# Two GIN layers on sorted edges: sums of six edge chunks in PSUM and masked adds in SBUF, in place of scatter-adds to DRAM

## Chip, core and metric

The kernel runs on one core of a Trainium2 chip. Its engines work side by side, each through its own queue in order: PE (TensorE, with its weight loads shown as PEld), DVE (VectorE), ACT (ScalarE), POOL (GpSimd) and SP (SyncE, which here only issues DMAs). DMAs are issued by SP, ACT and POOL, and the data is moved by 16 DMA engines. The metric is the device time of one execution in microseconds (us); lower is better.

## The reference

A graph with 6250 nodes and 100000 edges. Each of two layers adds to every node the rows of the nodes that have an edge to it, then applies two dense layers. At the end stand a residual and a layernorm. Everything is float32.

```python
# x [6250, 256], src and dst [100000]; dst is sorted
dst = jnp.minimum((6250 * jax.random.uniform(key, (100000,)) ** 2.0).astype(jnp.int32), 49999)
_o = jnp.argsort(dst, stable=True); src = src[_o]; dst = dst[_o]

def _gin_agg(h, src, dst, eps, n_nodes):
    agg = jax.ops.segment_sum(h[src], dst, num_segments=n_nodes)
    return (1.0 + eps) * h + agg

h = _gin_agg(x, src, dst, eps1, n)          # width 256
h = jax.nn.relu(h @ W1a + b1a)              # 256 -> 512
h = jax.nn.relu(h @ W1b + b1b)              # 512 -> 512
h = _gin_agg(h, src, dst, eps2, n)          # width 512
h = jax.nn.relu(h @ W2a + b2a)              # 512 -> 512
x = _layernorm(x + h @ W2b + b2b)           # 512 -> 256
```

The destinations are squares of uniform numbers times 6250, so low node numbers have many edges and high ones few.

## The kernel before

The edges are cut into 782 chunks of 128, one edge in each partition. Edge p * 782 + c stands in partition p of chunk c, so the 128 edges of a chunk are far apart in the list. The program has four stages, one behind the other: aggregate, mlp, aggregate, mlp.

**aggregate** (L171) works on four chunks (GRP) at a time. For each chunk, POOL issues an indirect DMA that gathers the 128 source rows from DRAM into a tile g (L176), six chunks (AHEAD) ahead of their use. PE transposes the chunk's destinations into a PSUM tile pt (L189), and DVE compares them with themselves to get a selection matrix sel (L193): 1 where two edges share a destination. PE multiplies sel with g into pm (L215), which adds up the rows of a chunk that share a destination. ACT copies pm to m (L217), and POOL issues a second indirect DMA that adds m to an accumulator in DRAM (L218); only the first edge of a destination adds to the true row, the others go to spare rows. Which row each edge adds to is worked out on DVE in the first aggregation (L201 to L209) and used again in the second. There are four accumulators (NACC) per layer, so that scatters can overlap.

**mlp** (L225) takes 512 nodes (BLK) at a time: SP loads the four accumulators' rows (part, L235), DVE adds them up (L238), PE transposes them (L241), and the two matrix products follow (ph at L249, po at L258). In the first layer the result goes to DRAM as h1 (L269), and, scaled, as the seed of the second accumulator (L272). In the second come residual and layernorm (L274 to L290).

Before the first aggregation the accumulators are filled: SP writes the seeds (L142), and ACT issues the zero fills (L115, L121) for all accumulators of both layers. ACT's copies at L217 stand behind these issues in ACT's queue. x stays in SBUF for the seed and the residual.

The order within each engine's queue is set by the framework's scheduler from the order in the code, the tile pools' buffer counts (bufs) and the dependences.

Of the kernel before, what the change touches and what calls it, by code (L numbers as in the profile page):

```python
# [11 lines left out]
ALU = mybir.AluOpType  # L12

P = 128
NACC = 4    # independent accumulators in DRAM, so that scatter-adds overlap
# [3 lines left out]
EPS_LN = 1e-5  # L19


@with_exitstack
def tile_gin_residual_layernorm(
# [32 lines left out]
    PAD = N                         # the row to which padding edges add  # L56
    ROWS = -(-(N + 1 + P) // P) * P  # nodes, padding row, a spare row per partition
# [3 lines left out]
    edge = ctx.enter_context(tc.tile_pool(name="edge", bufs=3))  # L61
    dense = ctx.enter_context(tc.tile_pool(name="dense", bufs=2))
    psum = ctx.enter_context(tc.tile_pool(name="psum", bufs=2, space=bass.MemoryType.PSUM))

    acc1 = [dram.tile([ROWS, D], F32, name=f"acc1_{k}") for k in range(NACC)]
    acc2 = [dram.tile([ROWS, H], F32, name=f"acc2_{k}") for k in range(NACC)]
    h1 = dram.tile([N, H], F32, name="h1")

# [1 line left out]
    srcs = const.tile([P, NCH], I32, name="srcs")  # L70
    dsti = const.tile([P, NCH], I32, name="dsti")
    nc.gpsimd.memset(srcs, 0)
    nc.gpsimd.memset(dsti, PAD)
    full = E // NCH
    for t, a in ((srcs, src), (dsti, dst)):
        nc.sync.dma_start(t[:full], a[: full * NCH].rearrange("(p c) -> p c", c=NCH))
        if E > full * NCH:
            nc.sync.dma_start(  # L78
                t[full : full + 1, : E - full * NCH],
                a[full * NCH :].rearrange("(p c) -> p c", p=1),  # L80
            )
# [3 lines left out]
    before = const.tile([P, P], F32, name="before")  # 1 where column < partition  # L85
    nc.gpsimd.memset(before, 1.0)
    nc.gpsimd.affine_select(
        out=before, in_=before, pattern=[[-1, P]], compare_op=ALU.is_gt, fill=0.0,
        base=0, channel_multiplier=1,
    )  # L90
    spare = const.tile([P, 1], F32, name="spare")
    nc.gpsimd.iota(spare, pattern=[[0, 1]], base=N + 1, channel_multiplier=1,
                   allow_small_or_imprecise_dtypes=True)

    dstf = const.tile([P, NCH], F32, name="dstf")
    nc.vector.tensor_scalar(dstf, dsti, float(PAD), None, op0=ALU.min)  # L96
    move = const.tile([P, NCH], F32, name="move")    # from the destination to the spare row
    nc.vector.tensor_scalar(move, dstf, -1.0, spare, op0=ALU.mult, op1=ALU.add)
    rows = const.tile([P, NCH], I32, name="rows")    # the row to which an edge adds

# [6 lines left out]
    zeros = const.tile([P, 1600], F32, name="zeros")  # L107
    nc.vector.memset(zeros, 0.0)

    def zero(acc, width):  # L110
        flat = acc.rearrange("(p r) d -> p (r d)", p=P)
        total = ROWS // P * width
        for o in range(0, total, 1600):
            n = min(1600, total - o)
            nc.scalar.dma_start(flat[:, o : o + n], zeros[:, :n])  # L115

    def zero_spare(acc, width):
        n = ROWS - N
        for r in range(0, n, P):
            m = min(P, n - r)  # L120
            nc.scalar.dma_start(acc[N + r : N + r + m, :], zeros[:m, :width])  # L121

    xs = const.tile([P, NT, D], F32, name="xs")
    for n0 in range(0, N, BLK):
        nb = min(BLK, N - n0)
        t0 = n0 // P
        g = nb // P
        if g:
            nc.sync.dma_start(
                xs[:, t0 : t0 + g, :], x[n0 : n0 + g * P, :].rearrange("(t p) d -> p t d", p=P)  # L130
            )
        if nb > g * P:
            nc.sync.dma_start(xs[: nb - g * P, t0 + g, :], x[n0 + g * P : n0 + nb, :])

    zero_spare(acc1[0], D)
    for a in acc1[1:]:
        zero(a, D)
    for t in range(NT):
        m = min(P, N - t * P)
        s = dense.tile([P, D], F32, tag="seed1", name="seed1", bufs=3)  # L140
        nc.vector.tensor_scalar(s[:m], xs[:m, t, :], e1[:m, 0:1], None, op0=ALU.mult)
        nc.sync.dma_start(acc1[0][t * P : t * P + m, :], s[:m])  # L142

# [1 line left out]
    def weight(w, kk, width, name):  # L145
        t = const.tile([P, kk, width], F32, name=name)
        nc.sync.dma_start(t, w.rearrange("(k p) f -> p k f", p=P))
        return t
# [17 lines left out]
    for a in acc2[1:]:  # L166
        zero(a, H)
    zero_spare(acc2[0], H)

# [1 line left out]
    def aggregate(table, width, accs, find_rows):  # L171
        gathered = {}

        def gather(c):
            g = edge.tile([P, width], F32, tag="g", name="g", bufs=AHEAD + 2)
            nc.gpsimd.indirect_dma_start(  # L176
                out=g, out_offset=None, in_=table,
                in_offset=bass.IndirectOffsetOnAxis(ap=srcs[:, c : c + 1], axis=0),
            )
            gathered[c] = g  # L180

        for c in range(min(AHEAD, NCH)):
            gather(c)
        for c0 in range(0, NCH, GRP):
            n = min(GRP, NCH - c0)
            cs = slice(c0, c0 + n)
            pt = psum.tile([P, GRP, P], F32, tag="pt", name="pt")
            for i in range(n):
                nc.tensor.transpose(  # L189
                    pt[:, i, :], dstf[:, c0 + i : c0 + i + 1].to_broadcast([P, P]), ident  # L190
                )
            sel = edge.tile([P, GRP, P], F32, tag="sel", name="sel")
            nc.vector.tensor_tensor(  # L193
                sel[:, :n, :], pt[:, :n, :], dstf[:, cs].unsqueeze(2).to_broadcast([P, n, P]),
                op=ALU.is_equal,
# [14 lines left out]
            for i in range(n):  # L210
                c = c0 + i
                if c + AHEAD < NCH:
                    gather(c + AHEAD)
# [111 lines left out]
```

## Time and profile before

| | |
|---|---|
| timed runs, median of 3 | 5891.14 us (5888.76 to 5893.97) |
| profiled execution, its span | 5891.6 us |
| busy: PE, DVE, ACT, POOL | 3258.7, 876.9, 864.8, 4031.6 us |
| moved by DMA | 802.48 MB, 136 GB/s over the span |
| gathers and scatters (software queue q0) | 325312 packets, 615.19 MB |
| mean granted TensorE clock | 0.601 of full speed |

The page of the profile shows the span in 40 slices, with each engine's busy share in tenths; the groups of instructions by line give count, mean duration in ns, and the idle time ahead of them with what ended it. The timeline lists instructions in order of time, with the idle time of the engine ahead of each. A matrix product in float32 appears as two MATMUL records. The granted clock is the share of full speed that the hardware gave TensorE.

### The profile page before, as it was taken

How to read it: one execution, taken by the hardware profiler on the slowest of the kernel's cores; microseconds unless marked ns; L12 is line 12 of the kernel's file. 1: busy time of each engine (PE TensorE's matmuls, PEld its weight loads, DVE VectorE, ACT ScalarE, POOL GpSimd, SP SyncE). 2: the span in 40 equal slices, each digit the busy share in tenths (PEclk: the TensorE clock that was granted, in tenths of full speed). 3: DMA queues.
4: the chain of work that ended last, by engine and by line, in shares of the span. 5: the costliest groups of instructions: out<-in, count | busy, mean ns of one | idle time of the engine just before them, and what ended most of it. 6: DMA issues, size and time to landing. Idle time of an engine off the chain costs nothing.

```text
span 5891.6 us, 29066 instructions
## 1 busy us (share of the span) xinstructions
PE 3258.7 (55%) x6394; PEld 1396.1 (24%) x6394; DVE 876.9 (15%) x3186; ACT 864.8 (15%) x1768; POOL 4031.6 (68%) x3139
## 2 busy tenths in 40 slices
PE   0244444444444444446976666666666666666688
PEld 0122222222222222222432222222222222222254
DVE  1011111111111111112410000000000000000354
ACT  0011111111111111111211111111111111111111
POOL 0388888888888888883038888888888888888300
PEclk7555555555555555557986666655666655655699
DMA  7855555555555555555559999999999999999753
GB/s 275 289 82 82 82 83 83 82 83 82 82 82 82 83 82 83 82 82 137 185 135 166 165 165 165 165 165 165 166 165 166 165 165 165 166 165 165 182 170 112
DMA packets 430637, 802.48 MB, mean 136 GB/s; under 512 B 62132, under 2 KB 206768, under 8 KB 430466
## 3 DMA queue, kind: packets, MB, share of 16 engines
q0 software_dynamic: 325312, 615.19, 60.7%
q1 hardware_dynamic: 71740, 93.57, 5.3%
q10 hardware_dynamic: 33414, 91.86, 4.0%
q8 instruction: 56, 0.92, 0.1%
q14 instruction: 115, 0.94, 0.1%
HBM read 395.04 MB, written 405.34 MB: 136 GB/s over the span
## 4 chain that ended last, share of the span: by engine, by line
DMA 66%; issue 13%; PE 8%; POOL 7%; DVE 3%; ACT 1%; SPq 1%; ACTq 0%; POOLq 0%; DVEq 0%
DMA g<-in_x_dram,srcs 34%; DMA g<-h,srcs 18%; DMA acc<-m,rows 7%; POOL acc L218 5%; DMA part<-acc 4%; PE pm L215 4%; PE po L258 3%; PE ph L249 2%; POOL g L176 2%; DMA acc<-seed 2%; DVE part L238 1%; DMA acc<-zeros 1%; ACT m L217 1%; DMA xs<-in_x_dram 0%; SPq L78 0%
## 5 line engine op out<-in xcount | busy, mean ns | idle before, releaser
L215 PE MATMUL pm<-g,sel 128*128 128x256 f32 (+1 forms) x3128 | 2352.0, 854 | 2464.0 <-DMA g<-in_x_dram,srcs 1377.6
L218 POOL DMA_INDIRECT acc<-m,rows x1564 | 2462.9, 1575 | 648.9 <-issue 332.0
L215 PEld LDWEIGHTS pm<-g,sel 128*128 128x128 f32 x3128 | 751.4, 298 | 3776.5 <-ACT m L217 3397.8
L217 ACT COPY m<-pm 128x256 f32<-128x256 f32 (+1 forms) x1564 | 748.5, 479 | 4213.5 <-DMA acc<-m,rows 2903.9
L176 POOL DMA_INDIRECT g<-h,srcs x782 | 771.6, 987 | 550.9 <-issue 471.8
L176 POOL DMA_INDIRECT g<-in_x_dram,srcs x782 | 794.6, 1016 | 279.8 <-DMA g<-in_x_dram,srcs 125.3
L193 DVE TENSOR_TENSOR sel<-pt,dstf 128x512 f32<-128x512 f32 x392 | 270.2, 690 | 4450.1 <-PE pm L215 4439.7
L189 PE MATMUL pt<-ident,dstf 128*128 128x128 f32 x1564 | 406.8, 413 | 53.0 <-DVE dstf L96 51.5
L189 PEld LDWEIGHTS pt<-ident,dstf 128*128 128x128 f32 x1564 | 338.7, 225 | 323.0 <-issue 301.3
L238 DVE TENSOR_TENSOR part<-part 128x256 f32<-128x256 f32 (+2 forms) x294 | 163.6, 557 | 335.0 <-DMA part<-acc 331.6
L249 PE MATMUL ph<-zt,w2a_s 128*128 128x512 f32 (+1 forms) x416 | 191.8, 623 | 12.7 <-DVE zt L244 12.7
L201 DVE SCALAR_TENSOR_TENSOR scr<-sel,before 128x128 f32<-128x128 f32 x782 | 181.6, 287 | 6.6
L258 PE MATMUL po<-w1b_s,ht 128*128 128x512 f32 (+1 forms) x392 | 172.3, 597 | 3.5 <-DVE h1t L266 3.5
L249 PEld LDWEIGHTS ph<-zt,w2a_s 128*128 128x128 f32 x416 | 83.2, 209 | 114.7 <-issue 98.5
L258 PEld LDWEIGHTS po<-w1b_s,ht 128*128 128x128 f32 (+1 forms) x392 | 74.7, 191 | 98.4 <-issue 92.3
L258 PE MATMUL po<-w2b_s,ht 128*128 128x256 f32 (+1 forms) x392 | 90.8, 389 | 6.6 <-DVE y L276 6.6
L241 PE MATMUL pt<-ident,part 128*128 128x128 f32 (+1 forms) x294 | 49.2, 295 | 80.6 <-DVE part L238 47.3
L249 PE MATMUL ph<-zt,w1a_s 128*128 128x512 f32 (+1 forms) x208 | 89.2, 582 | 4.7 <-DVE zt L244 4.7
L258 PEld LDWEIGHTS po<-w2b_s,ht 128*128 128x128 f32 (+1 forms) x392 | 76.1, 195 | 24.2 <-DVE y L276 8.2
L253 ACT ACTIVATE ht<-ph,b2a_s 128x512 f32<-128x512 f32 (+1 forms) x52 | 34.4, 661 | 202.1 <-PE ph L249 188.4
L201 DVE DVE_READ_ACCUMULATOR scr<-sel,before 128x1 f32 x782 | 63.6, 81 | 0.0
L241 PEld LDWEIGHTS pt<-ident,part 128*128 128x128 f32 (+1 forms) x294 | 34.3, 147 | 101.5 <-issue 57.5
(34 smaller groups left out, 412.6 us busy)
## 6 DMA issues: line engine op xcount, KB each, us to landing
acc<-zeros ACTq DMA_DIRECT2D x72, 800.0 KB
part<-acc SPq DMA_DIRECT2D x192, 256.0 KB
acc<-m,rows POOLq DMA_INDIRECT x1564
part<-acc SPq DMA_DIRECT2D x192, 128.0 KB
g<-in_x_dram,srcs POOLq DMA_INDIRECT x782
g<-h,srcs POOLq DMA_INDIRECT x782
h<-h1r ACTq DMA_DIRECT2D x48, 256.0 KB
acc<-seed ACTq DMA_DIRECT2D x48, 256.0 KB
```

Of the source, the lines that this page charges most:

```text
L176: nc.gpsimd.indirect_dma_start(out=g, out_offset=None, in_=table, in_offset=bass.IndirectOffsetOnAxis(ap=srcs[:, c : c + 1], axis=0),)
L189: nc.tensor.transpose(pt[:, i, :], dstf[:, c0 + i : c0 + i + 1].to_broadcast([P, P]), ident)
L193: nc.vector.tensor_tensor(sel[:, :n, :], pt[:, :n, :], dstf[:, cs].unsqueeze(2).to_broadcast([P, n, P]), op=ALU.is_equal,)
L201: nc.vector.scalar_tensor_tensor(scr, sel[:, i, :], 1.0, before, op0=ALU.mult, op1=ALU.mult, accum_out=earlier[:, i : i + 1],)
L215: nc.tensor.matmul(ps, sel[:, i, :], gathered.pop(c), start=True, stop=True)
L217: nc.scalar.copy(m, ps)
L218: nc.gpsimd.indirect_dma_start(out=accs[c % NACC][:, :], out_offset=bass.IndirectOffsetOnAxis(ap=rows[:, c : c + 1], axis=0), in_=m, in_of ...
L238: nc.vector.tensor_tensor(parts[0][:m], parts[0][:m], p[:m], op=ALU.add)
L241: nc.tensor.transpose(pt[:, k, :m], parts[0][:m, k * P : (k + 1) * P], ident[:m, :m])
L249: nc.tensor.matmul(ph[:, :nb], wa[:, k, f * P : (f + 1) * P], zt[:, k, :nb], start=(k == 0), stop=(k == kk - 1),)
L253: nc.scalar.activation(ht[:, f, :nb], ph[:, :nb], AF.Relu, bias=ba[:, f : f + 1])
L258: nc.tensor.matmul(po[:m], ht[:, f, o : o + m], wb[:, f, :], start=(f == 0), stop=(f == KH - 1),)
```

## The change

The kernel gets a second scheme for edges that come sorted by destination with about the known distribution, and a test that decides between it and the old scheme at run time.

- The edges are now placed in order: chunk c holds edges 128 c to 128 c + 127. Small pieces of src and dst are loaded, transposed by PE and copied to srcs and dsti (L138 to L160).
- Six chunks (768 edges) are a group; there are 131 groups. A node's slot is its number modulo 128. If a group's destinations span at most 127 nodes, each slot stands for one node.
- places() works out from formulas, for each group, which tiles of 128 nodes it can reach (lo to hi). The masks (L190) say, for each group, slot and reachable tile, whether the slot's node lies in it.
- A flag counts groups that span too many nodes or lie outside places(). All engines read it and branch (L571 and L572): to ordered() if it is 0, else to general(), which is the old scheme with its zero fills, DRAM accumulators and scatters.
- In ordered(), aggregation and dense layers of a layer are one loop over the groups. For a group DVE makes one selection (L353: slot against a row of 0 to 127 that lies in PSUM). PE adds the six chunks up in one PSUM tile pm (L362). DVE adds pm, times the mask, to each reachable tile's accumulator in SBUF (L368; 2 to 4 tiles, 365 adds per layer). The accumulators (10 buffers) start as scaled rows of the table (L284, L285).
- As soon as no later group can reach four tiles, their dense block is queued, and pump() puts one step of it behind every second chunk (L365). Gathers run 20 chunks ahead (AHEAD), with 22 buffers.
- x is no longer kept in SBUF; the residual is loaded again (L388). Weights are loaded from ACT's queue.

```diff
-NACC = 4    # independent accumulators in DRAM, so that scatter-adds overlap
-GRP = 4     # edge chunks whose selection matrices are built together
-AHEAD = 6   # gathers in flight ahead of the arithmetic
+GRP = 6
+AHEAD = 20
+TILES = 4
+SIGMAS = 6.5
...
+def places(N, E):
+    step = GRP * P
+    groups = -(-E // step)
+
+    def node(e, side):
+        dev = SIGMAS * math.sqrt(max(e, 1) * max(1.0 - e / E, 0.0)) + 24
+        return N * min(max((e + side * dev) / E, 0.0), 1.0) ** 2
+
+    lo = [int(node(step * g, -1)) // P for g in range(groups)]
+    hi = [min(int(node(step * g, 1)), N - 1) // P + 1 for g in range(groups)]
+    return lo, hi
...
+        own = prep.tile([P, NG], F32, tag="own", name="own", bufs=1)
+        nc.vector.scalar_tensor_tensor(own, wb, part, tb, op0=ALU.is_gt, op1=ALU.add)
+        nc.vector.tensor_tensor(own, own, lowest, op=ALU.subtract)
+        for k in range(KM):
+            nc.vector.tensor_scalar(mask[:, k, :], own, float(k), None, op0=ALU.is_equal)
...
-    zero_spare(acc1[0], D)
-    for a in acc1[1:]:
-        zero(a, D)
...
-    for a in acc2[1:]:
-        zero(a, H)
-    zero_spare(acc2[0], H)
...
+            def seed(t):
+                m = rows(t)
+                a = edge.tile([P, width], F32, tag="acc", name="acc", bufs=10)
+                if m < P:
+                    nc.vector.memset(a, 0.0)
+                nc.sync.dma_start(a[:m], table[t * P : t * P + m, :])
+                nc.scalar.activation(a[:m], a[:m], AF.Copy, scale=scale[:m])
+                acc[t] = a
...
+            def gather(c):
+                g = edge.tile([P, width], F32, tag="g", name="g", bufs=AHEAD + 2)
+                nc.gpsimd.indirect_dma_start(
+                    out=g, out_offset=None, in_=table,
+                    in_offset=bass.IndirectOffsetOnAxis(ap=srcs[:, c : c + 1], axis=0),
+                )
...
+                    pt = psum.tile([P, kk, P], F32, tag="pt", name="pt", bufs=1)
...
+                    nc.scalar.copy(zt[:, :, i * P : i * P + m], pt[:, :, :m])
+                    yield
...
+            for g in range(NG):
+                while seeded < min(hi[g] + 2, NT):
+                    seed(seeded)
+                    seeded += 1
+                c0 = g * GRP
+                n = min(GRP, NCH - c0)
+                sel = edge.tile([P, GRP, P], F32, tag="sel", name="sel")
+                nc.vector.tensor_tensor(
+                    sel[:, :n, :], iop.unsqueeze(1).to_broadcast([P, n, P]),
+                    slot[:, c0 : c0 + n].unsqueeze(2).to_broadcast([P, n, P]), op=ALU.is_equal,
+                )
+                pm = psum.tile([P, width], F32, tag="pm", name="pm")
+                for i in range(n):
+                    c = c0 + i
+                    if c + AHEAD < NCH:
+                        gather(c + AHEAD)
+                    nc.tensor.matmul(
+                        pm, sel[:, i, :], gathered.pop(c), start=(i == 0), stop=(i == n - 1)
+                    )
+                    if i % 2:
+                        pump()
+                for t in range(lo[g], min(hi[g], NT - 1) + 1):
+                    nc.vector.scalar_tensor_tensor(
+                        acc[t], pm, mask[:, t - lo[g], g : g + 1], acc[t],
+                        op0=ALU.mult, op1=ALU.add,
+                    )
+                done = lo[g + 1] if g + 1 < NG else NT
+                while blocks < NT and min(blocks + TILES, NT) <= done:
+                    todo.append(block(blocks))
+                    blocks += TILES
+            while todo:
+                pump()
...
+    strays = nc.values_load(flag[0:1, 0:1])
+    with tc.If(strays < 1) as choice:
+        with ExitStack() as inner:
+            ordered(inner)
+    with choice.Else():
+        with ExitStack() as inner:
+            general(inner)
```

How the instructions stand in the queues, at three places. First POOL's queue of before, from the first gathers on (g is a gathered tile, acc_0 to acc_3 the accumulators in DRAM):

```order
L176 DMA g<-in_x_dram,srcs 128x256 x10
L218 DMA acc_0_69<-m,rows 6400x256
L218 DMA acc_1_70<-m,rows 6400x256
L176 DMA g<-in_x_dram,srcs 128x256
L218 DMA acc_2_71<-m,rows 6400x256
```

And POOL's queue of the change, from its last setting-up instruction to the start of the general branch (h_60 is h1 in DRAM):

```order
L602 ISA
L290 DMA g<-in_x_dram,srcs 128x256 x775
L290 DMA g<-h_60,srcs 128x512 x782
L572 UNCONDITIONAL_BRANCH
L409 MEMSET before 128x128
L461 DMA g<-in_x_dram,srcs 128x256
```

A gather and a scatter took turns; now the gathers of both layers follow each other with nothing between, and the scatters stand only behind the branch.

Second, DVE's queue of before in the first aggregation (numbers tell the tiles apart; earlier counts the edges of a chunk with the same destination ahead of an edge):

```order
L193 TENSOR_TENSOR sel_3387<-pt_3382,dstf_96 128x512
L201 SCALAR_TENSOR_TENSOR scr_3390,earlier_3389<-sel_3387,before_91 128x128
L201 SCALAR_TENSOR_TENSOR scr_3392,earlier_3389<-sel_3387,before_91 128x128
L201 SCALAR_TENSOR_TENSOR scr_3394,earlier_3389<-sel_3387,before_91 128x128
L201 SCALAR_TENSOR_TENSOR scr_3396,earlier_3389<-sel_3387,before_91 128x128
L206 SCALAR_TENSOR_TENSOR off_3398<-earlier_3389,move_98 128x4
L209 TENSOR_TENSOR rows_100<-off_3398,dstf_96 128x4
```

And DVE's queue of the change at the start of the first layer (sel_425 belongs to pm_427, sel_448 to pm_450, and so on):

```order
L353 TENSOR_TENSOR sel_425<-iop_374,slot_64 128x768
L353 TENSOR_TENSOR sel_448<-iop_374,slot_64 128x768
L353 TENSOR_TENSOR sel_471<-iop_374,slot_64 128x768
L368 SCALAR_TENSOR_TENSOR acc_416<-pm_427,mask_181,acc_416 128x256
L368 SCALAR_TENSOR_TENSOR acc_419<-pm_427,mask_181,acc_419 128x256
L353 TENSOR_TENSOR sel_494<-iop_374,slot_64 128x768
```

A selection no longer needs PE's transposes, and it stands three groups ahead of the adds of its own group.

Third, PE's queue of before in the first mlp (ph and po are the two products) :

```order
L258 MATMUL po<-w1b_s,ht 128x512 x16
L241 MATMUL pt<-ident,part 128x128 x8
L249 MATMUL ph<-zt,w1a_s 128x512 x8
L258 MATMUL po<-w1b_s,ht 128x512 x16
L241 MATMUL pt<-ident,part 128x128 x8
```

And PE's queue of the change from the end of the first layer into the second:

```order
L362 MATMUL pm<-g,sel 128x256 x8
L306 MATMUL pt<-ident,acc 128x128 x8
L315 MATMUL ph<-zt,w1a_s 128x512 x8
L325 MATMUL po<-w1b_s,ht 128x512 x16
L306 MATMUL pt<-ident,acc 128x106 x2
L315 MATMUL ph<-zt,w1a_s 128x106 x8
L325 MATMUL po<-w1b_s,ht 106x512 x4
L362 MATMUL pm<-g,sel 128x512 x236
L306 MATMUL pt<-ident,acc 128x128 x4
L362 MATMUL pm<-g,sel 128x512 x2
L306 MATMUL pt<-ident,acc 128x128 x4
L362 MATMUL pm<-g,sel 128x512 x2
```

Dense blocks are now cut into steps between pairs of chunks, but the last full block of a layer and the block of 106 rows stand undivided behind the layer's last chunk.

More of the change, by code (lines that the diff above doesn't have):

```diff
@@ L1 @@
+import math
 from contextlib import ExitStack
@@ L71, in tile_gin_residual_layernorm @@
-    dsti = const.tile([P, NCH], I32, name="dsti")
+    srcs = const.tile([P, NCP], I32, name="srcs")
+    dsti = const.tile([P, NCP], I32, name="dsti")
+    dstf = const.tile([P, NCP], F32, name="dstf")
+    slot = const.tile([P, NCP], F32, name="slot")
     nc.gpsimd.memset(srcs, 0)
[L73 to L81, printed above, removed]
+    nc.gpsimd.memset(dsti, 0)
@@ L83, in tile_gin_residual_layernorm @@
     ident = const.tile([P, P], F32, name="ident")
     make_identity(nc, ident)
[L85 to L92, printed above, removed]
-                   allow_small_or_imprecise_dtypes=True)
@@ L95, in tile_gin_residual_layernorm @@
[L95 to L99, printed above, removed]
+    iota = const.tile([P, P], F32, name="iota")
+    nc.gpsimd.iota(iota, pattern=[[1, P]], base=0, channel_multiplier=0,
+                   allow_small_or_imprecise_dtypes=True)
+    part = const.tile([P, 1], F32, name="part")
@@ L105, in tile_gin_residual_layernorm @@
     nc.vector.tensor_scalar(e1, e1, 1.0, None, op0=ALU.add)
[L107 to L133, printed above, removed]
-    zero_spare(acc1[0], D)
-    for a in acc1[1:]:
-        zero(a, D)
[L138 to L142, printed above, removed]
     def weight(w, kk, width, name):
         t = const.tile([P, kk, width], F32, name=name)
-        nc.sync.dma_start(t, w.rearrange("(k p) f -> p k f", p=P))
+        nc.scalar.dma_start(t, w.rearrange("(k p) f -> p k f", p=P))
         return t
```

456 lines of the change are left out of this document (338 added, 118 removed).

## The prediction

> **What bounds the kernel now.** I read the page's top first, then the groups by line, then the timeline of one engine.
>
> ```profile
> span 5891.6 us, 29066 instructions
> ...
> PE 3258.7 (55%) x6394; PEld 1396.1 (24%) x6394; DVE 876.9 (15%) x3186; ACT 864.8 (15%) x1768; POOL 4031.6 (68%) x3139
> ...
> POOL 0388888888888888883038888888888888888300
> PEclk7555555555555555557986666655666655655699
> ...
> L218 POOL DMA_INDIRECT acc<-m,rows x1564 | 2462.9, 1575 | 648.9 <-issue 332.0
> L176 POOL DMA_INDIRECT g<-h,srcs x782 | 771.6, 987 | 550.9 <-issue 471.8
> L176 POOL DMA_INDIRECT g<-in_x_dram,srcs x782 | 794.6, 1016 | 279.8 <-DMA g<-in_x_dram,srcs 125.3
> ```
>
> POOL is the fullest engine. Its row of slices shows four stages: two long ones at 8 tenths (the aggregations) and a gap after each (the dense layers). 8 tenths looks like room to spare; the timeline of POOL says otherwise:
>
> ```profile
> 4000.46 0.99 POOL L176 DMA_INDIRECT g<-h,srcs  x1 [0.30 <-issue]
> 4001.75 1.58 POOL L218 DMA_INDIRECT acc<-m,rows  x1 [0.30 <-issue]
> 4003.64 0.99 POOL L176 DMA_INDIRECT g<-h,srcs  x1 [0.30 <-issue]
> ```
>
> One gather, one scatter, each behind 0.30 us that no other engine causes: 0.99 + 0.30 + 1.58 + 0.30 = 3.17 us a chunk, and the next gather starts 3.18 us after the first. POOL is full. 782 chunks x 3.18 = 2487 us for each aggregation, 4974 of the 5891.6 us. The chain of waits blames "DMA g" for half of the span, but a gather is late there because POOL issues it late.
>
> ```profile
> 30.45 1.15 POOL L176 DMA_INDIRECT g<-in_x_dram,srcs  x1 [27.24 <-DMA srcs<-in_src_dram]
> ...
> 228.28 1.28 ACT L217 ACT_TABLE_LOAD   x1 [228.28 <-DMA acc<-zeros]
> ...
> 1000.00:2640.00 1640.00, 722.69 (x1544) 371.97 (x1544) 250.28 (x1414) 190.89 (x514) 1326.76 (x1029) 0.50 0.52 82
> 2700.00:3050.00 350.00, 294.71 (x749) 132.57 (x748) 135.68 (x299) 71.09 (x113) 29.81 (x25) 0.93 0.53 161
> 3150.00:5450.00 2300.00, 1462.59 (x2168) 487.87 (x2169) 125.08 (x181) 423.12 (x723) 1859.66 (x1447) 0.61 0.91 165
> ```
>
> The other stages: 228 us in which ACT, which issues the zero fills, cannot copy a first chunk, and the dense layers, in which POOL has almost nothing to do (ahead of layer 2 it is idle for 313.18 us, in a row below). (Columns of the window rows: PE, PEld, DVE, ACT, POOL busy, then granted clock, DMA share, GB/s.) The profiled span lies inside the timed runs (5888.76 to 5893.97), so the sum is made against 5891.6.
>
> **The change, part by part. Scatters (1564) go:** 1564 x (1.58 + 0.30) = 2940 us of POOL time. What is late next is POOL still, with one gather a chunk. The trace has such a stretch, the first gathers of layer 2:
>
> ```profile
> 3026.39 1.01 POOL L176 DMA_INDIRECT g<-h,srcs  x1 [313.18 <-issue]
> ...
> 3030.24 0.95 POOL L176 DMA_INDIRECT g<-h,srcs  x1 [0.30 <-issue]
> 3031.49 0.95 POOL L176 DMA_INDIRECT g<-h,srcs  x1 [0.30 <-issue]
> 3032.74 0.94 POOL L176 DMA_INDIRECT g<-h,srcs  x1 [0.30 <-issue]
> ...
> 3030.25 5.95 PE L215 MATMUL pm<-g,sel 128*128 128x512 f32 x8 [9.51 <-DMA g<-h,srcs]
> ...
> 3030.00:3036.00 6.00, 5.75 (x8) 2.20 (x8) 0.00 (x0) 1.75 (x3) 4.54 (x5) 0.60 0.75 215
> ```
>
> Alone, a gather comes every 1.25 us; with the mean duration of layer 1 it would be 1.016 + 0.30 = 1.32. I take 1.27, near the row that has no scatters in it, and keep 1.25 and 1.32 as ends: 782 x 1.27 = 993 us a layer (978 to 1032). The DMA engines carried this at 215 GB/s and a share of 0.75, so they are not full, though not far from it. A gather lands 3030.25 - 3026.39 = 3.9 us after its issue starts; 20 ahead at 1.27 us is 25 us of cover, so the latency shows once a layer.
>
> ```profile
> L287 DVE TENSOR_SCALAR o<-y,mv,rs 128x256 f32<-128x256 f32 x48 | 19.5, 407 | 0.0
> ```
>
> This last step of the layernorm, from SBUF to SBUF, now runs beside gathers. [...] No row of this trace shows such an overlap, and the sum leaves it out.
>
> **TensorE.** The masks and accumulators replace the transposes of L189; six chunks now add up in one PSUM tile. The matmuls themselves stay, and the dense ones now stand between them. Their full-clock rates come from the dense layers:
>
> ```profile
> 2776.20 7.13 PE L249 MATMUL ph<-zt,w1a_s 128*128 128x512 f32 x16 [0.42 <-DVE zt L244]
> 2783.17 13.90 PE L258 MATMUL po<-w1b_s,ht 128*128 128x512 f32 x32
> ...
> 5552.10 7.07 PE L258 MATMUL po<-w2b_s,ht 128*128 128x256 f32 x32
> 5559.01 1.04 PE L241 MATMUL pt<-ident,part 128*128 128x128 f32 x8
> 5563.62 15.70 PE L249 MATMUL ph<-zt,w2a_s 128*128 128x512 f32 x32 [0.78 <-DVE zt L244]
> ```
>
> A matmul is two records, so 512 columns cost 13.90/16 = 0.87 us and 256 columns 7.07/16 = 0.44. A block of four tiles costs 7.1 + 13.9 + 8 x 0.13 = 22 us in layer 1 and 15.7 + 7.1 + 16 x 0.13 = 25 us in layer 2. From the formulas of places(), blocks become due after groups 38, 54, 65, 75, 84, 92, 99, 106, 112, 118, 124, 129 and 130 of 131.
>
> Layer 1: over the shortest regular interval, six groups, POOL needs 36 x 1.27 = 46 us and PE 36 x 0.44 + 22 = 38. POOL stays the bound. After the last gather the order of PE leaves 3.9 us of landing, a full block and the 106-row one: 22 + 7 + about 5 for hand-overs (each tile's transpose waits some 0.4 us and a copy, as the 0.42 at 2776.20), then bias, relu and the write to h1, about 6. Layer 1: 993 + 44 = 1037 us.
>
> Layer 2: PE needs 6 x 0.87 = 5.2 us of a group's 7.6, so it gains 2.4 us a group and loses 25 a block. With ten groups or fewer between blocks it no longer keeps up, which is so from group 75. So 75 x 7.62 = 572 us by POOL, then by PE 56 x 5.2 + 9 x 25 + 8 = 524. Landing 4, hand-overs of the last blocks 10, and the end:
>
> ```profile
> 5886.52 0.27 ACTq L290 DMA_DIRECT2D out_dram<-o  x1
> ```
>
> From that issue to the end of the span is 5 us, with the layernorm of one tile ahead of it 8. 572 + 524 + 22 = 1118; I add 22 (4% of PE's part) for waits between blocks, as PE is only 294.71 of 350 us busy in the dense window above. Layer 2: 1140.
>
> **VectorE** gets a selection of 128x768 a group and 365 masked adds a layer (from places()).
>
> ```profile
> L193 DVE TENSOR_TENSOR sel<-pt,dstf 128x512 f32<-128x512 f32 x390 | 269.4, 691 | 4426.9 <-PE pm L215 4416.6 <-PE pt L189 10.4
> ...
> L238 DVE TENSOR_TENSOR part<-part 128x512 f32<-128x512 f32 x144 | 99.2, 689 | 164.7 <-DMA part<-acc 163.0
> ...
> L238 DVE TENSOR_TENSOR part<-part 128x256 f32<-128x256 f32 x144 | 61.1, 424 | 146.2 <-DMA part<-acc 144.5
> ```
>
> From 424 ns for 256 columns and 690 for 512, 768 take about 0.96 us. A group of layer 2 costs 0.96 + 3 x 0.69 = 3.0 us of its 7.6: hidden behind gathers. Without that cover it would be 131 x 3.0 = 393 us a layer. The adds are a new wait: PE may not refill one of two pm tiles before they are done, but the order has each selection three groups ahead of its use, and two groups are 15 us. The seeds and copies on ACT and the loads of seeds on SP (10 accumulators) are a few per cent of a layer each: nothing.
>
> **Start.** The zero fills, seeds to DRAM and 228 us go. The new preparation loads 16 small pieces, transposes them, works out masks and a flag, and every engine reads the flag before it branches. From below: the first gather cannot come much earlier than now, 30 us (row at 30.45). From above: three times that, 90. I take 45, nearer to the row: the loads are no larger than the old ones, and the small steps behind them make the difference.
>
> Sum: 45 + 1037 + 1140 = 2222, forecast **2220 us**. The removed parts are 228 - 45 at the start, two dense stages that now lie under gathers, and 1.9 us a chunk.
>
> **The rivals.**
>
> A. PE does not get its clock.
>
> ```profile
> PE pm L215 <- DMA g<-h,srcs: 877.6, 661, 9.5
> ```
>
> In the second aggregation PE waits 661 times for a gather, 1.3 us in the mean, and the granted clock is 0.61, in the first 0.50. If the new layers got these, PE work of 782 x 0.44 + 12.2 x 22 = 612 us would take 1224, and 782 x 0.87 + 12.2 x 25 = 985 would take 1615: with 45 and some 60 of tails 2940 us. Against it: PE that is kept full is granted 0.93 to 1.0 (dense window), and a PE that falls behind is full. Chance 0.06.
> [...]
>
> B. The DMA engines bound layer 2. At 165 GB/s, where they show 0.91, a gather of 262 KB takes 1.59 us: 1243 + 60 for layer 2, 2385 in all. For it: random 2 KB rows, and seeds, residual and output beside them. Against: 215 GB/s at 0.75 with gathers alone. Chance 0.10.
>
> C. Waits in line: adds, layernorm steps and copies stand in one order on DVE and ACT, and PE waits for a pm, po or pt tile that is queued behind them. At 3 us a group in half of the groups: 400 us, 2600. The order speaks against more. Chance 0.12.
>
> D. POOL alone is the bound: 45 + 2 x 978 + 44 + 35 = 2080 to 2110. It needs PE never to fall behind in layer 2. Chance 0.08.
>
> E. Slower: the general branch is taken. Its place is the branch after the flag; it decides as soon as one group of 768 edges spans more than 127 nodes or starts outside its row of places(). Then the old scheme runs behind the preparation: 5892 + 45 = 5937 us. The destinations that setup_inputs makes are sorted, the widest group spans 96 nodes, and none lies outside. Chance 0.01; the same rival is "the change does not do what it says".
>
> **How the numbers follow.** Forecast 0.63 (2150 to 2320), A 0.06, B 0.10, C 0.12, D 0.08, E 0.01. The range takes in the forecast, D's ends, B and the nearer half of C: 2090 to 2500; A, the far half of C and E stay out, about 0.13. A measurement can tell 0.2%, 12 us, from no change. Faster 0.985, same 0.003, slower 0.012 (E, with a little for what nobody thought of).
>
> **What would show it.** Right: POOL rows with only gathers, 1.25 to 1.32 us apart, through layer 1; PE's largest releaser is "DMA g" in layer 1 and the first 60% of layer 2, and POOL waits for PE in the last 40%; the two layers at about 1040 and 1140 us. Wrong: a granted clock under 0.7 in layer 2's second half (A); gathers landing late at a DMA share over 0.9 (B); PE waiting on DVE or ACT for hundreds of us (C); the lines of the general branch in the groups (E).

## The result

| | runs | median us | range us |
|---|---|---|---|
| before | 4 | 5889.95 | 5888.45 to 5893.97 |
| changed | 4 | 2533.15 | 2530.84 to 2538.84 |

The ratio is 0.4302, with a 95% interval of 0.4295 to 0.4308. The time lies 313 us above the forecast and 33 above the top of its range. One thing has to be said at once: in the sitting of this result (a sitting is one set of runs on one chip) the other engines started late on TensorE's results, and in five of eight later sittings they did not; in the three of these five in which the same kernel ran, it takes 2134 to 2136 us.

### The profile page after: what moved, and what is told of

Its sections match the earlier page's. It is cut to its first block, busy times and chain, and to the rows that moved or that the text cites. A ratio compares the mean times of both kernels' runs of the same rounds, so it can differ in the third digit from the quotient of the medians.

```text
span 2537.1 us, 16073 instructions
## 1 busy us (share of the span) xinstructions
PE 1798.0 (71%) x4848; PEld 979.8 (39%) x4848; DVE 773.6 (30%) x1492; ACT 218.4 (9%) x402; POOL 1482.7 (58%) x1576
## 4 chain that ended last, share of the span: by engine, by line
PE 51%; another core or an unknown queue 31%; issue 9%; DVE 5%; DMA 2%; ACT 1%; POOL 0%; SPq 0%; DVEq 0%; POOLq 0%; ACTq 0%
PE pm L362 30%; PE ph L315 10%; PE po L325 9%; DVE acc L368 3%; PE pt L306 2%; DVE sel L353 2%; ACT zt L309 1%; POOL g L290 0%; DMA g<-h,srcs 0%; DMA raw<-in_src_dram 0%; DMA g<-in_x_dram,srcs 0%; DMA h<-h1r 0%; DMA raw<-in_dst_dram 0%; DMA acc<-h 0%
## 5 line engine op out<-in xcount | busy, mean ns | idle before, releaser
L362 PE MATMUL pm<-g,sel 128*128 128x256 f32 (+1 forms) x3128 | 1261.2, 553 | 406.7 <-DVE acc L368 239.6
L290 POOL DMA_INDIRECT g<-h,srcs x782 | 740.7, 947 | 549.7 <-PE pm L362 258.4
L362 PEld LDWEIGHTS pm<-g,sel 128*128 128x128 f32 x3128 | 669.3, 221 | 932.2 <-issue 535.3
L290 POOL DMA_INDIRECT g<-in_x_dram,srcs x782 | 739.0, 945 | 405.5 <-PE pm L362 145.5
L368 DVE SCALAR_TENSOR_TENSOR acc<-pm,mask,acc 128x256 f32<-128x256 f32 (+1 forms) x730 | 409.4, 612 | 1563.1 <-PE pm L362 852.3
L306 PE MATMUL pt<-ident,acc 128*128 128x128 f32 (+1 forms) x294 | 66.1, 343 | 269.4 <-issue 158.2
L353 DVE TENSOR_TENSOR sel<-iop,slot 128x768 f32<-128x768 f32 (+1 forms) x262 | 247.0, 943 | 0.0
L309 ACT COPY zt<-pt 128x256 f32<-128x256 f32 (+2 forms) x98 | 46.8, 477 | 1614.2 <-remote 1137.1
L306 PEld LDWEIGHTS pt<-ident,acc 128*128 128x128 f32 (+1 forms) x294 | 43.3, 173 | 324.9 <-issue 204.2
L315 PEld LDWEIGHTS ph<-zt,w1a_s 128*128 128x128 f32 x208 | 40.8, 206 | 68.6 <-issue 49.0
L285 ACT ACTIVATE acc<-acc,e 128x512 f32<-128x512 f32 (+1 forms) x98 | 59.7, 615 | 85.6 <-DMA acc<-in_x_dram 38.9
```

Source lines behind the costliest of these rows:

```text
L285: nc.scalar.activation(a[:m], a[:m], AF.Copy, scale=scale[:m])
L290: nc.gpsimd.indirect_dma_start(out=g, out_offset=None, in_=table, in_offset=bass.IndirectOffsetOnAxis(ap=srcs[:, c : c + 1], axis=0),)
L306: nc.tensor.transpose(pt[:, k, :m], a[:m, k * P : (k + 1) * P], ident[:m, :m])
L309: nc.scalar.copy(zt[:, :, i * P : i * P + m], pt[:, :, :m])
L315: nc.tensor.matmul(ph[:, :nb], wa[:, k, f * P : (f + 1) * P], zt[:, k, :nb], start=(k == 0), stop=(k == kk - 1),)
L353: nc.vector.tensor_tensor(sel[:, :n, :], iop.unsqueeze(1).to_broadcast([P, n, P]), slot[:, c0 : c0 + n].unsqueeze(2).to_broadcast([P, n, P ...
```

## The profile after

First the page of the changed kernel's profiled run: span, busy times, POOL and the granted clock in 40 slices, and the costliest groups.

```profile
span 2537.1 us, 16073 instructions
...
PE 1798.0 (71%) x4848; PEld 979.8 (39%) x4848; DVE 773.6 (30%) x1492; ACT 218.4 (9%) x402; POOL 1482.7 (58%) x1576
...
POOL 4666666666666666562466666565656655555540
PEclk9676778777887888888978889988988998999999
...
L362 PE MATMUL pm<-g,sel 128*128 128x256 f32 (+1 forms) x3128 | 1261.2, 553 | 406.7 <-DVE acc L368 239.6
L290 POOL DMA_INDIRECT g<-h,srcs x782 | 740.7, 947 | 549.7 <-PE pm L362 258.4
L290 POOL DMA_INDIRECT g<-in_x_dram,srcs x782 | 739.0, 945 | 405.5 <-PE pm L362 145.5
```

The scatters are gone, and a gather takes 0.945 us instead of 1.016. No engine is full: POOL fell from 68% to 58%. A gather behind a gather needs 0.945 + 0.30, so 782 of them need 974 us a layer. POOL's idle time ahead of layer 1's gathers is 405.5 us, 171 more than 782 times 0.30: there it mostly waits for TensorE, which had not yet given back a buffer of g (the 258.4 and 145.5 us in the rows hold some of the 0.30 us steps, too). TensorE in turn waits 239.6 us for VectorE's adds. The view of waits (total us, times, longest) says whom VectorE waited for:

```profile
DVE acc L368 <- PE pm L362: 852.3, 156, 28.7
DVE acc L368 <- remote: 579.4, 61, 28.0
...
POOL g L290 <- PE pm L362: 403.8, 435, 3.5
...
PE pm L362 <- DVE acc L368: 239.6, 64, 14.4
```

TensorE waits for VectorE, VectorE for TensorE. ("remote" stands where the semaphore's event came, but no instruction's record ends shortly before it.) The timeline shows how both can be so. Two rows of TensorE and two of VectorE in layer 2 (start, duration, operation, idle time ahead of it):

```profile
1354.74 5.74 PE L362 MATMUL pm<-g,sel 128*128 128x512 f32 x13
1371.93 12.95 PE L362 MATMUL pm<-g,sel 128*128 128x512 f32 x24 [11.46 <-issue]
...
1350.22 1.41 DVE L368 SCALAR_TENSOR_TENSOR acc<-pm,mask,acc 128x512 f32<-128x512 f32 x2 [2.88 <-PE pm L362]
...
1370.47 1.41 DVE L368 SCALAR_TENSOR_TENSOR acc<-pm,mask,acc 128x512 f32<-128x512 f32 x2 [17.98 <-remote]
```

The first of the 13 records at 1354.74 is the last of its group and ends at 1355.33; the other 12 are the next group, and end at 1360.48. VectorE, idle for 18 us, starts the first group's adds at 1370.47, 15 us behind its last record, and only then does TensorE go on, at 1371.93, into the pm tile that these adds freed. The first of the two adds waits for nothing but TensorE's semaphore. So the records say that the sum is done, and the semaphore says so 15 us later. (The ends of matmul records are modelled, so the trace can't say whether the sum itself or only its signal was late.) I matched the 262 groups of the two layers: in 106 the first add starts over 5 us behind the group's last matmul record, 27.5 us at most. None of these 106 has a product of a dense block between its matmuls. Of the 67 groups that have one, 59 are followed by their add within 0.1 us.

The trace also lacks semaphore events: it holds 13471, where the same program leaves 33567 in e5 below. Of TensorE's 2154 signals 1819 are there, of VectorE's 1389 only 940, and most of what is missing tells of landings of DMAs. The events of TensorE that are there carry a pattern. Their distances in this trace from 45.2 us on, and the same in units of 0.70 us:

```
us     2.47  4.89  11.20  11.20  5.62  2.79  2.12  0.04  1.37  4.20
/0.70   3.5   7.0   16.0   16.0   8.0   4.0   3.0   0.1   2.0   6.0
```

Of all distances over 0.6 us, 51% are within 8% of 0.70 us from a whole multiple of it (16% would be chance). For the account by steps below, the first and last gather of layer 1 and the first of layer 2:

```profile
27.88 1.10 POOL L290 DMA_INDIRECT g<-in_x_dram,srcs  x1 [6.77 <-DVE sel L353]
...
1164.73 0.94 POOL L290 DMA_INDIRECT g<-in_x_dram,srcs  x1 [0.30 <-issue]
1233.70 0.94 POOL L290 DMA_INDIRECT g<-h,srcs  x1 [68.02 <-DMA h<-h1r]
```

## The experiments

**First sitting after the result's: three theories on the late adds (e1 to e4).** (Where the expectations speak of "the first sitting", they mean the result's.) Theory 1: two pm tiles are too few for them. Theory 2: TensorE's clock, or its idle gaps, make them late. Theory 3: VectorE and GpSimd block each other. All four kernels read the counter row iota from SBUF, to free a bank.

```diff
-        iop = psum.tile([P, P], F32, tag="iop", name="iop", bufs=1)
-        nc.vector.tensor_copy(iop, iota)
+        iop = iota                                            # e1, e2, e3, e4
...
-                pm = psum.tile([P, width], F32, tag="pm", name="pm")
+                pm = psum.tile([P, width], F32, tag="pm", name="pm", bufs=3)   # e2, e3
...
-AHEAD = 20
+AHEAD = 32                                                    # e3
...
+        dz = psum.tile([P, 512], F32, tag="dz", name="dz", bufs=1)   # e4
...
+                    if not todo:                              # e4
+                        w = 256 if width == D else 128
+                        nc.tensor.matmul(dz[:, :w], ident, w1a_s[:, 0, :w], start=True, stop=True)
                     if i % 2:
                         pump()
```

> Only the counter row is moved: the selection on VectorE reads iota from SBUF and not from its copy in PSUM, which frees one PSUM bank and is the control for the next two kernels. Theory 1 (two pm tiles are too few, because VectorE learns some 10 us late that a group's sum is complete) and theory 2 (TensorE's clock): no change, 2533 us within 15. Theory 3 (VectorE and GpSimd block each other on SBUF): a selection that now reads only SBUF makes it worse, 2560 us or more, with selections longer than 0.95 us.

> As e1, with a third pm tile in the freed bank. Theory 1: TensorE no longer stands still until the adds two groups back are done; a third tile covers a delay of up to some 15 us, so gathers in layer 1 come back to 1.25 to 1.30 us apart and the time falls by 150 to 300 us, to 2230 to 2380. Theory 2 (clock) and theory 3: less than 30 us, 2500 to 2535.

> As e2, with 34 gather buffers and gathers 32 chunks ahead instead of 22 and 20. If GpSimd is held back because late completions keep gather buffers occupied, and by dense blocks of 22 to 25 us, it gains on e2: 40 to 100 us. If the pm tiles are all that matters: as e2 within 15 us.

> As e1, pm still two tiles; where no dense block is under way TensorE runs one extra matmul behind each chunk's (identity x a piece of a weight, 256 columns in layer 1, 128 in layer 2, into a bank that nobody reads), 0.44 and 0.22 us at full clock. Theory 2, that the thinly filled TensorE is the cause (low granted clock, or completions that come late while it is idle between chunks): the add follows the last record of its group at once, as it does beside dense blocks, gathers in layer 1 come 1.25 to 1.30 us apart, and the time falls by 150 to 300 us although TensorE does more. Theory 1 with a delay that has nothing to do with idle TensorE: no gain, or up to 100 us lost to the extra work.

Measured: 2202.9, 2203.0, 2201.4 and 2226.0 us (4 runs each). The control itself, e1, is 330 us under the result, and in none of the four traces is an add late: the largest distance is 0.8 us. Taken alone, e1 would say that a counter row in PSUM costs 330 us. But the result's time and e1's come from two sittings, and can't be compared until the changed kernel has run beside e1's.

**Second: the changed kernel again, and where the row lies (e5 to e8).** e5 has no edit. e6 keeps the PSUM copy in bank 0 but reads iota from SBUF. e7 reads the copy, which now lies in bank 7. e8 is e6 with an extra read of PSUM that nothing depends on:

```diff
+                scr = edge.tile([P, GRP, P], F32, tag="scr", name="scr")       # e8
+                nc.vector.tensor_copy(scr, held.unsqueeze(1).to_broadcast([P, GRP, P]))
                 pm = psum.tile([P, width], F32, tag="pm", name="pm")
```

> The changed kernel itself, once more beside the others. If the step from 2533 to 2203 us in e1 is the kernel's: 2533 within 10. If the chip made it: near 2203.

> Selection reads iota from SBUF as in e1, but the PSUM copy is still made and keeps bank 0, so that pm, pt, ph and po lie in the banks of the changed kernel (1 to 7). Theory P (VectorE's reads of a PSUM bank in every selection are the cause): 2203 us within 10, adds right behind their groups. Theory B (the place of pm and the others in PSUM is the cause): 2533 us, adds some 10 us late.

> Selection reads the PSUM copy as in the changed kernel, but the copy lies in bank 7 and pm, pt, ph and po in banks 0 to 6, as in e1. Theory P: 2533 us within 30, late adds. Theory B: 2203 us within 10.

> As e6, and once a group VectorE copies the PSUM tile, spread to 128x768, to a scratch tile in SBUF that nobody reads: the read without anything that depends on it. Theory P, by the read alone: late adds and 2400 us or more. If the read harms only because the selection hangs on it, or theory B is right: 2203 to 2225 us or as e6 (VectorE has 1 us more work in 7.6).

Measured: 2134.8, 2200.3, 2135.2 and 2197.3 us. e5, the unchanged program, is 398 us under the result; its ratio to the kernel before is 0.3621 (0.3615 to 0.3628). So what was different in the result's sitting, and not the program, made the 398 us, and the place of the row makes 66 us with the other sign (e6 against e5). Theory P and theory B both fall as causes of e1's gain: the bank doesn't matter (2134.8 and 2135.2 us in e5 and e7, 2202.9 and 2200.3 in e1 and e6), and a read of PSUM does no harm (2197.3 us in e8, 2200.3 in e6). No kernel that reads iota from SBUF ran in a sitting that is known to have late adds, so the runs don't show whether it would have them there. What the row costs in SBUF is in e1's page and timeline:

```profile
L289 POOL DMA_INDIRECT g<-in_x_dram,srcs x782 | 780.1, 998 | 244.7 <-issue 152.6
...
206.62 0.95 POOL L289 DMA_INDIRECT g<-in_x_dram,srcs  x1 [0.30 <-PE pm L361]
207.87 1.13 POOL L289 DMA_INDIRECT g<-in_x_dram,srcs  x1 [0.30 <-PE pm L361]
...
207.24 0.95 DVE L352 TENSOR_TENSOR sel<-iota,slot 128x768 f32<-128x768 f32 x1
```

The gather that meets the selection (207.24 to 208.19) takes 1.13 us, the one ahead of it 0.95. In e1's trace the 347 gathers that overlap a selection take 1.18 us in the mean, all others 0.946; in e5's trace, where a selection has one operand in PSUM, both kinds take 0.946 to 0.947. e6, in e5's sitting, has the row in SBUF too: the means over all gathers of layers 1 and 2 are 0.993 and 1.004 us there, 0.946 and 0.947 in e5. So a selection with both operands in SBUF lengthens the gathers that it meets, and the copy of iota in PSUM is what avoids it; by what path the two meet the traces don't show. Theory 3 falls as the cause of the late adds: in layer 1 of the result a gather takes 0.945 us and a selection 0.947, as in e5 (0.946 and 0.947), so neither engine lengthens the other's work there.

The page and the timeline of e5, to be read against the result's:

```profile
span 2132.1 us, 16073 instructions
...
POOL 4777777777777777776277777777777777666640
...
L290 POOL DMA_INDIRECT g<-in_x_dram,srcs x782 | 739.4, 946 | 245.1 <-issue 139.8
```

```profile
28.15 1.10 POOL L290 DMA_INDIRECT g<-in_x_dram,srcs  x1 [7.27 <-DVE sel L353]
...
208.43 0.70 PE L362 MATMUL pm<-g,sel 128*128 128x256 f32 x2 [0.51 <-DMA g<-in_x_dram,srcs]
209.76 0.70 PE L362 MATMUL pm<-g,sel 128*128 128x256 f32 x2 [0.64 <-DMA g<-in_x_dram,srcs]
...
210.50 0.87 DVE L368 SCALAR_TENSOR_TENSOR acc<-pm,mask,acc 128x256 f32<-128x256 f32 x2 [5.38 <-PE pm L362]
...
1004.48 0.95 POOL L290 DMA_INDIRECT g<-in_x_dram,srcs  x1 [0.30 <-PE pm L362]
1051.17 0.94 POOL L290 DMA_INDIRECT g<-h,srcs  x1 [45.73 <-DMA h<-h1r]
```

The group's last matmul record ends at 210.46 and the add starts at 210.50. POOL idles 245.1 us in layer 1, which is 0.30 a gather and little else: (1004.48 - 28.15) / 781 = 1.250 us a gather without a break. Of the distances of TensorE's semaphore events 7% are near a multiple of 0.70 us.

**Third to fifth (e9 to e14).** The changed kernel twice more; e4's extra matmuls with the row in PSUM (one po tile less, to free a bank) in e10 and e14; three pm tiles and one po tile (e11); gathers 32 ahead (e12).

> The changed kernel a third time, in another sitting. If the 398 us between 2533 and 2135 go with the chip or its state at that time: one of these two times again, with late adds (median over 1 us behind the last record of their group in layer 1) at 2533 and none at 2135. If the time simply varies from sitting to sitting: something between.

> The changed kernel with e4's extra matmuls behind each chunk where no dense block is under way (and one po tile instead of two, to free a bank). In a sitting with late adds: if they come late because TensorE idles between chunks, the adds follow at once and the time falls from 2533 to 2140 to 2250; if not, 2533 or more. In a sitting without: 2135 to 2175, since TensorE has 0.88 us of 1.25 to do for a chunk of layer 1 and 1.09 of 1.25 in layer 2.

> The changed kernel with three pm tiles and one po tile. In a sitting with late adds: theory 1 (two pm tiles are too few for adds that come 10 us late) gives 2230 to 2400 us; if the completions of TensorE are late for every user of them (gather buffers, transposes too), 2450 to 2540. In a sitting without late adds: 2135 within 15, TensorE waits only 13 us for adds there.

> The changed kernel with 34 gather buffers and gathers 32 chunks ahead. In a sitting with late adds: 2533 within 30 if pm is what holds TensorE, 2450 or less if the gather buffers are. In a sitting without: layer 1 as it is (1.25 us a gather without a break), the last quarter of layer 2 (1.40 us a gather, held by TensorE) no faster, 2120 to 2135.

> The changed kernel a fourth time. 2533 within 10 with late adds, if the state of the first sitting comes back; 2135 within 5 without.

> The kernel of e10 beside it. If e13 has late adds: 2175 to 2250 if they hang on an idle TensorE, 2500 or more if not. If e13 has none: 2176 within 5 as in e10.

Measured: 2133.6, 2176.0, 2139.7, 2136.4, 2135.6 and 2178.6 us. No add is late in any of them. More tiles and buffers gain nothing; the extra work costs 42 us (e10 against e9) although it lifts the granted clock from 0.90 to 0.99. So with sums that are reported at once, pm tiles, gather buffers and clock are not what bounds this kernel.

**Sixth to eighth: the late adds come back (e15 to e18).** e15 has extra matmuls only in layer 2, so that its layer 1 tells the state; e16 has three pm tiles, 34 gather buffers and one po tile; e17 is the changed kernel; e18 has so much extra work that TensorE is the bound by the estimate in its expectation, 1.31 us a chunk.

```diff
                     if not todo:                                       # e10, e14
-                        w = 256 if width == D else 128
+                        w = 512 if width == D else 256                 # e18
```

> Extra matmuls behind the chunks only in layer 2 (128 columns, where no dense block is under way), one po tile. If the state of the first sitting is back, layer 1 takes about 1200 us with adds some 10 us late; layer 2 then takes about 1100 us with adds at once if the lateness hangs on an idle TensorE, 1300 if not. If the state is not back: layer 1 some 1025 us, 2135 to 2160 in all.

> Three pm tiles, gathers 32 chunks ahead in 34 buffers, one po tile. In a sitting with late adds: if the lateness costs time only through buffers that it keeps occupied, a third pm tile covers 7 us more of it and the gather buffers 15 us more, 2200 to 2400; if TensorE itself gets less done then, 2500 to 2560. In a sitting without: 2135 to 2142, as e11 and e12.

> The changed kernel a fifth time: 2530 to 2575 with adds some 10 us late and gathers 1.40 us apart in the first quarters, if the state of the last two sittings holds; 2135 within 5 if not.

> The kernel of e10 with extra matmuls of 512 columns in layer 1 and 256 in layer 2: 0.44 + 0.87 and 0.87 + 0.44 = 1.31 us of work for a chunk that is gathered every 1.25, so TensorE is the bound and soon never waits. If e17 is slow: 2210 to 2300 and no late adds if the lateness hangs on a TensorE that waits; 2550 or more if it is there whatever TensorE does. If e17 is not: 2210 to 2260.

Measured: 2579.8, 2573.1, 2543.5 and 2557.6 us (2 runs each). e16 lies 13 us above even the higher of its two ranges: the buffers gain nothing. All runs of the changed kernel and its variants with iop in PSUM, in one table; the two columns of the pace are 196 gathers at the head of each layer, that of the late adds the mean distance from a group's last matmul record to its first add:

| run | what it is | us | us a gather, layer 1 / 2 | add late by, layer 1 / 2 | events on 0.70 us |
|---|---|---|---|---|---|
| result | changed | 2533.2 | 1.41 / 1.40 | 6.0 / 4.4 | 51% |
| e17 | changed | 2543.5 | 1.41 / 1.40 | 6.0 / 4.4 | 50% |
| e16 | 3 pm, 34 g | 2573.1 | 1.40 / 1.40 | 8.7 / 7.4 | 48% |
| e15 | extra work in layer 2 | 2579.8 | 1.43 / 1.43 | 5.9 / 3.7 | 55% |
| e18 | extra work, TensorE full | 2557.6 | 1.43 / 1.42 | 3.0 / 2.4 | 50% |
| e5, e9, e13; e7 | changed; row in bank 7 | 2133.6 to 2135.6 | 1.25 / 1.25 | 0.0 / 0.0 | 6 to 7% |
| e11, e12 | 3 pm; 34 g | 2139.7, 2136.4 | 1.25 / 1.25 | 0.0 / 0.0 | 6% |
| e10, e14 | extra work | 2176.0, 2178.6 | 1.25 / 1.25 | 0.0 / 0.0 | 5% |

There are two states and nothing between. In the late state a chunk takes 1.40 to 1.43 us ahead of the first dense blocks, in both layers, though the matmul of layer 2 costs twice that of layer 1 (0.87 us and 0.44, from the prediction's rows of the dense layers). More buffers leave the pace as it is and let the adds fall further behind: 8.7 us instead of 6.0. That is what a backlog would do in front of something that passes one chunk in 1.40 us. Theory 1 falls with it. Theory 2 falls with e18, where TensorE hardly idles and adds are still late by 3.0 and 2.4 us in the mean. (Its pace of 1.43 says less, since its own work takes TensorE 1.31 us a chunk by the expectation, and it didn't run without the late adds.) The same stretch of layer 1 (100 to 300 us) in e18, in e16 and in e5, in this order, with columns as in the prediction:

```profile
100.00:300.00 200.00, 187.97 (x563) 106.89 (x562) 41.48 (x73) 0.00 (x0) 132.44 (x141) 0.98 0.32 92
```

```profile
100.00:300.00 200.00, 97.17 (x270) 72.44 (x270) 41.09 (x73) 0.88 (x2) 130.00 (x138) 0.67 0.32 90
```

```profile
100.00:300.00 200.00, 165.27 (x328) 71.34 (x328) 47.78 (x85) 2.64 (x6) 151.28 (x161) 0.65 0.37 107
```

e18 has TensorE busy for 188 of 200 us at a clock of 0.98 and issues 141 gathers; e16 has 97 us at 0.67 and issues 138; e5, without the state, issues 161 at 0.65. So e16's pace isn't set by TensorE's work or clock (e5 goes faster at 0.65), by the DMA engines (a share of 0.32) or by VectorE (41 us of 200).

**What stays open** is what passes only one chunk in 1.40 us, and why it came in four sittings of nine. It isn't the chip as such: one chip showed it in e16 and not in e11 and e12. Nor is it the number of TensorE's signals: over the table's gathers of layer 1, e18 has 1.85 of them to a gather and the result 0.96, at 1.43 and 1.41 us.

One rival is untested, and the traces point to it. All five traces with late adds lack more than half of their semaphore events (13471 to 14718 are there); all 14 others of the changed kernel and its variants hold 33565 to 34515. Every run on record has a profiled span beside its time. So the recording of the events may itself hold the engines back, which no run shows; a run that nothing records would tell. The runs show that the lost events and the late adds come together, not which is the cause. Only one trace of before is kept. It is nearly whole (2261 of TensorE's 2311 signals), but was on record ahead of the prediction, so it doesn't tell what before leaves in a late sitting. A kernel with two chunks to a gather wasn't tried either.

## Why the prediction was right or wrong, point by point

The terms of the sum beside what the rows give. The first three come from the gathers quoted above; group 75's first matmul, found by counting twelve records a group, stands at 1925.1 us in the result's trace and at 1621.6 in e5's.

| term | forecast | result | e5 |
|---|---|---|---|
| start to the first gather | 45 | 27.9 | 28.2 |
| layer 1, first to last gather | 993 | 1136.9 | 976.3 |
| to the first gather of layer 2 | 44 | 69.0 | 46.7 |
| layer 2 to group 75 (572 + 4 landing) | 576 | 691.4 | 570.4 |
| group 75 to the end (524 + 10 + 8 + 22) | 564 | 612.0 | 510.5 |
| sum | 2222 | 2537.1 | 2132.1 |

- **The step that failed** is the pace: "Alone, a gather comes every 1.25 us ... I take 1.27". It priced a chunk by POOL alone, as long as TensorE's work fits beside it, and took it that TensorE gives buffers back as soon as its matmul is over. In the result's sitting that signal came late, and a chunk took 1.40 us at the head of the layers. Against the forecast that is +144 us in layer 1, +115 in layer 2 up to group 75, +25 in the wait between the layers and +48 behind group 75; the start gave 17 back. Against e5, the same program, the four are 161, 121, 22 and 102. Why the signal comes late stays open. The time of before did not give it away: a chunk took 3.18 us there, more than twice the 1.40 of the late state, and it is the same in all sittings to 0.1% (medians of 5889.95 to 5896.06).
- **Where the state is away, the mechanism holds** and the forecast is 85 us too high. The start was mis-sized by 17 us, the gather (1.25, the low end) by 17. The largest miss is TensorE's part of layer 2, 54 us. Two rows of windows of e5:

```profile
1054.00:1622.00 568.00, 524.18 (x1141) 190.44 (x1142) 215.60 (x333) 28.58 (x49) 429.72 (x455) 1.00 0.76 221
1622.00:2132.00 510.00, 497.17 (x1428) 255.51 (x1426) 238.07 (x456) 76.12 (x141) 308.39 (x326) 0.99 0.67 201
```

  TensorE takes over at about group 75, as forecast, and is then busy for 497 of 510 us. Half of the 54 us is work (524 forecast, 497 measured), half is idle time: 40 us were put down for it (22 between blocks, 10 for hand-overs, 8 for the end), and 13 came.
- **What was to show it**: POOL's gathers 1.25 to 1.32 us apart in layer 1, TensorE waiting there for gathers most of all. In e5 they are 1.25 apart, and of TensorE's 137.3 us of idle time ahead of layer 1's chunks 108.7 end with a gather; in the result's trace 123.6 of 243.3 end with VectorE's adds (by lines with one row a shape).
- **VectorE** is hidden as said: a selection takes 0.947 us (0.96 forecast), an add 0.745 and 0.478 (0.69 and 0.42 forecast, for 512 and 256 columns). The "three groups ahead of its use, and two groups are 15 us" held in e5, where TensorE waits 13.3 us for adds in all.
- **Rival A** (the clock) is refuted as a cause: a clock of 0.65 in layer 1 of e5 (100 to 300 us) goes with gathers at 1.25 us, and raising it to 0.99 (e10) gains nothing. TensorE's waits in e5's layer 1 are short: 0.51 and 0.64 us in the rows above, and the longest of its 204 waits for a gather is 2.7 us. What sets the clock there was not shown.
- **Rival B** (DMA) did not come: e5 moves 221 GB/s at a share of 0.76 and keeps 1.25 us a gather.
- **Rival C** (waits in line, 2600) has the nearest time, by luck, and its sign came true: TensorE waited 239.6 us for adds. Its mechanism did not: in the rows above nothing was queued ahead of the late adds on VectorE, which had been idle.
- **Rival D** (POOL alone, 2080 to 2110) is nearest where the state is away; TensorE's part at the end is most of what 2132 has over it. Its low end, 2080, lies outside the stated range of 2090 to 2500, which by the prediction takes in both of its ends.
- **Rival E** did not come; the ordered branch ran.
- **The layernorm beside gathers**, which the sum left out, cost nothing that shows: the 47 gathers that meet its last step in the result take 0.947 us in the mean, the others of layer 2 take 0.947 as well. What does cost time beside gathers is a selection with both operands in SBUF (1.18 us a gather instead of 0.946, in e1); the change avoids it by its copy of iota in PSUM.

## What to carry to other kernels

When one run of a change differs from a well-founded sum by hundreds of us, run the same kernel again beside the first experiment before believing either: here a control would have passed for a cure worth 330 us, and the true effect of its edit is 66 us the other way. Read whether an engine's consumers start when its records end: here the distance grew with the number of buffers, from 6.0 to 8.7 us in layer 1, as it would in front of a backlog. Count the semaphore events against the instructions that make them: a trace that lacks half of them may not show the kernel as it runs unrecorded. Where VectorE reads two operands beside GpSimd's gathers, try one of them in PSUM: for this kernel's selection that was worth 66 us (2134.8 in e5 against 2200.3 in e6).

## What the runs showed of the hardware that was not expected

- A state, in four of nine sittings and on one chip both there and away, in which half of the distances over 0.6 us between TensorE's signals lie near multiples of 0.70 us, more than half of all semaphore events are missing from the trace, chunk after chunk passes at 1.40 to 1.43 us instead of 1.25, and this kernel takes 2533 to 2544 us instead of 2134 to 2136. The kernel before, at 3.18 us a chunk, takes the same time to 0.1% in all sittings.
- A selection with both operands in SBUF lengthens a gather that it meets from 0.946 to 1.18 us (e1); with one operand in PSUM gathers take 0.946 to 0.947 us with it and without it (e5).
- A TensorE that is paced by gathers worked at a granted clock of 0.65 (e5, 100 to 300 us) and lost nothing by it: a chunk took 1.25 us there, and at a clock of 0.99 as well (e10).
